# Which 128 keys make a chunk: every second token of 256, or every 26th token of all

## The chip, the cores and the metric

The kernel runs on one core of one Trainium2 chip. A core has a matrix engine (TensorE, PE in the profile), a vector engine (VectorE, DVE), an engine for activation functions (ScalarE, ACT), a general one (GpSimd, POOL), a queue that issues transfers (SyncE, SP), and 16 DMA engines that move data between the device memory and the on-chip memory SBUF. TensorE writes its results to PSUM. The metric is the device time of the launch in microseconds (us); the median of three runs of the kernel before is 10094.3 us (10090.54 to 10097.2).

## What is computed

Two graph layers on 3327 tokens of 128 features. Layer 0 is a graph attention layer over the 0/1 matrix `adj`. Layer 1 carries nearly all of the time:

```python
q = (x @ Wq.T).reshape(d, n, h)          # d = 128, n = 3327 tokens, h = 8
k = (x @ Wk.T).reshape(d, n, h)
v = (x @ Wv.T).reshape(d, n, h)
a = einsum('dnh,dmh->dnm', q, k) * scale + adj + adj
a = softmax(a, axis=2)                   # over the keys m
out = einsum('dnm,dmh->dnh', a, v)
x = layernorm(x + out.reshape(n, h * d) @ Wo.T)
```

So there are 128 independent attentions ("heads" in this text), each with 3327 queries, 3327 keys and only 8 numbers per query, key and value. For each one a table of 3327 x 3327 scores is made, `2 * adj` is added (or its exponential multiplied in), every element goes through an exponential, and the result is multiplied by the values. The sum over keys does not depend on the order in which the keys are taken.

## The kernel before, in words

**Tiling of layer 1.** The heads are taken four at a time (`HG = 4`), in 32 groups `g`. In a group the queries are cut into 7 blocks `b` of 476 (the last of 472). In a block the keys are cut into `NT = 26` chunks of up to 128 keys, one key to each of the 128 partitions; 25 chunks have 128 keys and the last has 127 (`kr`). Keys on partitions and queries along the row make a score tile of 128 x 476 for each of the four heads. That is 32 x 7 x 26 = 5,824 chunks of four heads.

**Which tokens a chunk holds.** Chunk `i` holds the tokens `i, i + 26, i + 52, ...`: partition `p` has token `26 p + i`. The keys `k4` of a group lie in SBUF as 32 rows (for each head: 8 features and their rounding errors, each twice) of 3327 tokens, and `scores` (lines 136 to 143) takes the slice `k4[..., i::NT]` of them as the stationary operand of a matmul, one element in every 26. The values `v4` lie with keys on partitions: partition `p` holds the 26 tokens from `26 p` on, 9 numbers each (8 values and a one for the sum), which is one run of 936 bytes of device memory per partition and head (`values`, lines 693 to 697). The adjacency tile `at` of a stretch of three chunks (`want_adj`, lines 722 to 743) takes two or three neighbouring rows of the transposed `adj` for each partition, 476 numbers of each row. [...]the transfers of the last chunk are cut by `_cut` into 112, 15 and 1 partitions.

**Rounds.** A stretch of three chunks `(i, i+1, i+2)` is worked on in three rounds (`rounds`, line 885 on). In each round TensorE makes four score tiles (four matmuls of 32 x 128 weights, one for each quarter of the rows of the array, L137), then up to eight matmuls of side work, and then the products with the values of a chunk of four rounds ago (`products`, L906: four matmuls, which the profile shows as eight). Two ways lead from scores to weights. For a chunk in `times` (the first of each stretch) ScalarE takes the exponential straight from PSUM (L1104, two heads, 952 columns) and GpSimd multiplies by a factor tile made of `adj` (L1105). For the other two VectorE adds `adj` (L1107, two heads) and ScalarE takes the exponential of four heads at a time in SBUF (L936, 1904 columns); for the last two chunks of the block it takes two heads at a time (`late`, lines 1110 to 1118). Per stretch ScalarE thus has two activations of 952 columns and two of 1904.

**Buffers and order.** The order of every engine is written out by hand (`tc.manual_schedule`); each engine runs its list in order and waits on semaphores. The score tiles of chunks in `times` have one PSUM buffer (`pe`), the others two (`pd`), the accumulated product one (`pv`), the weights `e4` seven. An adjacency tile is asked for three stretches before its use (`AHEAD = 3`) and there are five of them. In the first group (`RAW`, 63 stretches) all three chunks of a tile are loaded from `adj`, and GpSimd turns the first into a factor (`make_factor`, L750), which is stored (`ftd`); from then on the factor is loaded (L731) and only the other two chunks come from `adj` (L740). The loads all go through SP's queue. The keys and values of the next group are loaded in the last 18 rounds of a group (`OPEN`): the list `parts` has four transfers of keys and three of values, and its k-th is issued in round `18 k / len(parts)` of these. For the first group the values are loaded from ScalarE's queue. Layer 0, the projections and the final result are woven in as side work on TensorE, VectorE and GpSimd (`work_tensor`, `work`); they keep their own order of tokens (`p * NT + i`), as does the path `general`, which is not taken with this data.

Of the kernel before, what the change touches and what calls it, by code (L numbers as in the profile page):

```python
# [17 lines left out]
P = 128  # L18
# [16 lines left out]
def _ap(t, offset, dims):  # L35
    return bass.AP(tensor=t.tensor, offset=t.offset + offset, ap=[list(d) for d in dims])


def _cut(n):

    if n % 16 == 0:
        return [(0, n)]
    c = (n - 1) // 16 * 16
    return [(a, b) for a, b in ((0, c), (c, n)) if b > a]
# [3 lines left out]
def kernel(  # L48
# [27 lines left out]
    nc = tc.nc  # L76
    N, D = x.shape
    H = wqT.shape[1]
    assert D == P
    NT = -(-N // P)  # L80
    G = N * D
    H1 = H + 1
    H4 = 4 * H
# [4 lines left out]
    HG = 4  # L88
    NG = D // HG

    FP = N // NT
    kr = [FP + (i < N - FP * NT) for i in range(NT)]
    assert FP == P - 1
    REST = N - FP * NT
# [16 lines left out]
    vd = dram.tile([G + 1, H1], F32, name="vd")  # L111
# [12 lines left out]
    where = {i: (i % 3 if NT % 3 != 1 or i < NT - 1 else 1) for i in range(NT)}  # L124
# [6 lines left out]
    eps = const.tile([P, 1], F32, name="eps")  # L131
    nc.vector.memset(eps, EPS)
    flag = const.tile([1, 1], I32, name="flag")
    ALL = {ENG.PE, ENG.Activation, ENG.DVE, ENG.Pool, ENG.SP}

    def scores(dst, k4, q4, i, r, j, nb, stop=True):
        nc.tensor.matmul(  # L137
            dst,
            k4[32 * j : 32 * j + H4, i::NT],
            q4[32 * j : 32 * j + H4, :nb],  # L140
            start=True,
            stop=stop,
        )


    def special():
        with ExitStack() as sx, tc.manual_schedule(engines=ALL):
            keep = sx.enter_context(tc.tile_pool(name="sx_keep", bufs=1))
            bg2 = sx.enter_context(tc.tile_pool(name="sx_bg2", bufs=2))
# [95 lines left out]
            def tick(all_=False):  # L245
                for p in pend:
                    p[0] -= 1
                while pend and (all_ or pend[0][0] <= 0):
                    pend.pop(0)[1]()
# [431 lines left out]
            def open_group(g):  # L681

                k4 = kp.tile([P, N], F32R, name="k4b")
                v4 = kp.tile([P, HG, VW], F32, name="v4b")
                nc.gpsimd.memset(v4[:, :, REST * H1 :], 0.0)

                def keys(j, engine=nc.sync):
                    engine.dma_start(
                        k4[32 * j : 32 * j + H4, :].bitcast(F32),
                        _ap(kT, (g * HG + j) * N, [[G, 2 * H], [0, 2], [1, N]]),  # L690
                    )

                def values(p0, p1, k, engine=nc.sync):
                    engine.dma_start(
                        v4[p0:p1, :, : k * H1],
                        _ap(vd, (g * HG * N + p0 * NT) * H1, [[NT * H1, p1 - p0], [N * H1, HG], [1, k * H1]]),
                    )

                parts = [lambda j=j, **kw: keys(j, **kw) for j in range(HG)]
                for p0, p1, k in [c + (NT,) for c in _cut(FP)] + [(FP, P, REST)]:  # L700
                    parts.append(lambda c=(p0, p1, k), **kw: values(*c, **kw))
                return k4, v4, parts

            def open_queries(g, b):
# [17 lines left out]
            def want_adj(n):  # L722

                if n >= len(stretches):
                    return
                g, b, m = stretches[n]
                a = adjs[n] = ap_.tile([P, 3, WB], F32, name="at")
                n0, _, w = exact[b]
                cs = stretch[m]
                if n >= RAW and cs[0] in times:  # L730
                    nc.sync.dma_start(a[:, 0, :w], ftd[b][m][:, :w])  # L731
                    cs = cs[1:]
                z = where[cs[0]]
                there = sum(i < REST for i in cs)
                parts = [(0, P, there)]
                if there < len(cs):
                    parts = [c + (len(cs),) for c in _cut(FP)] + [(FP, P, there)]
                for p0, p1, k in parts:
                    if k:
                        nc.sync.dma_start(  # L740
                            a[p0:p1, z : z + k, :w],
                            _ap(adjT, (p0 * NT + cs[0]) * N + n0, [[NT * N, p1 - p0], [N, k], [1, w]]),
                        )

            def make_factor(n):
                if n < min(RAW, len(stretches)) and stretch[stretches[n][2]][0] in times:
# [10 lines left out]
            with ExitStack() as st:  # L757
# [40 lines left out]
                for m in range(AHEAD):  # L798
                    want_adj(m)
# [86 lines left out]
            for m, st_ in enumerate(stretch):  # L886
                starts[len(rounds)] = m
                if len(st_) > 1:
                    i = st_[0]
# [173 lines left out]
            for g in range(NG):  # L1063
                k4, v4, _ = group
                for b in range(NBLK):
                    s = Block()
                    s.g, s.b, s.q4, s.k4, s.v4, s.left, s.e, added = g, b, queries[0], k4, v4, NT, {}, {}
                    w = s.w = exact[b][2]
                    for n, rnd in enumerate(rounds):
                        at = b * NR + n  # L1070
                        if n in starts:
                            m = (g * NBLK + b) * NST + starts[n]
                            want_adj(m + AHEAD)
                            a = adjs[m]
                        tick()
                        if g + 1 < NG:
                            if at == total - OPEN:
                                finish_to(("rows", reads[g + 1]), None)
                                tick(True)
                                group = open_group(g + 1)  # L1080
                            for k, f in enumerate(group[2]):
                                if at >= total - OPEN and at == total - OPEN + OPEN * k // len(group[2]):
                                    f()
                        if n == NR // 2 and (b + 1 < NBLK or g + 1 < NG):
                            queries = open_queries(g, b + 1) if b + 1 < NBLK else open_queries(g + 1, 0)
                        for j in range(HG):
                            if n == NR // 2 + j * (NR > 12) and (b + 1 < NBLK or g + 1 < NG):
                                queries[1](j)
                        sc = []
                        for i, h in rnd:  # L1090
                            sc.append((pe if i in times else pd).tile([P, 2, 512], F32, name="scb"))
                            for t in range(2):
                                scores(sc[-1][: kr[i], t, :w], s.k4, s.q4, i, kr[i], 2 * h + t, w)
                        work_tensor(g * total + at, n)
                        for (i, h), z in zip(rnd, sc):
                            r = kr[i]
                            if i not in s.e:
                                s.e[i] = sp.tile([P, HG, WB], F32, name="e4")
                                added[i] = 0
                            eh = s.e[i][:r, 2 * h : 2 * h + 2, :w]  # L1100
                            added[i] += 1
                            ah = a[:r, where[i], :w].unsqueeze(1).to_broadcast([r, 2, w])
                            if i in times:
                                nc.scalar.activation(eh, z[:r, :, :w], AF.Exp, scale=2.0)  # L1104
                                nc.gpsimd.tensor_tensor(eh, eh, ah, op=ALU.mult)  # L1105
                            else:
                                nc.vector.tensor_tensor(eh, z[:r, :, :w], ah, op=ALU.add)  # L1107
                        now = g * total + at
                        exp_late(now)
                        for i, h in rnd:  # L1110
                            if i in times:
                                continue
                            if NT % 3 == 2 and i == NT - 1:
                                late.append((now + 2, s, i, 2 * h, 2 * h + 2))
                            elif NT % 3 == 2 and i == NT - 3:
                                late.append((now + 1 + h, s, i, 2 * h, 2 * h + 2))
                            elif added[i] == 2 and (now + 1, s, i, 0, HG) not in late:
                                late.append((now + 1, s, i, 0, HG))
                        if n + 1 in starts or n + 1 == NR:
                            del adjs[m]  # L1120
                            make_factor(m + 1)
                        waiting.append((s, order[n]))
                        while len(waiting) > LAG:
                            products(*waiting.pop(0))
                        work(g * total + at, n)
# [386 lines left out]
```

## Time and profile before

| | |
|---|---|
| median of three runs | 10094.3 us (10090.54 to 10097.2) |
| span of the profiled execution, first to last instruction | 10090.1 us |
| median less span (what lies around the span, and the spread of runs) | 4.2 us |
| busy: PE / DVE / ACT / POOL | 9904.1 / 9357.3 / 9969.7 / 9204.1 us (98 / 93 / 99 / 91%) |
| weight loads (PEld) | 3839.3 us, of them 2527.0 us for the scores (23,296 loads of 295 ns mean) |
| transfers | 1728.28 MB, mean 171 GB/s; 1,183,646 packets |
| granted TensorE clock, mean | 0.996 |

The profiled execution gives no time of its own besides its span. A busy time is the union of an engine's instructions. Matmuls are pipelined, and the ends that the profile gives them are modelled, so that a PE at 98% is not shown to be at its limit. A weight load (PEld) fills the stationary operand and may overlap with matmuls that are already running. ACT's instructions overlap by some 0.1 us where they follow one another at once, so that busy times of its groups sum to more than the engine's. All engines but the queue are over 90% busy, and the shares alone do not tell which of them sets the pace.

### The profile page before, as it was taken

How to read it: one execution, taken by the hardware profiler on the slowest of the kernel's cores; microseconds unless marked ns; L12 is line 12 of the kernel's file. 1: busy time of each engine (PE TensorE's matmuls, PEld its weight loads, DVE VectorE, ACT ScalarE, POOL GpSimd, SP SyncE). 2: the span in 40 equal slices, each digit the busy share in tenths (PEclk: the TensorE clock that was granted, in tenths of full speed). 3: DMA queues.
4: the chain of work that ended last, by engine and by line, in shares of the span. 5: the costliest groups of instructions: out<-in, count | busy, mean ns of one | idle time of the engine just before them, and what ended most of it. 6: DMA issues, size and time to landing. Idle time of an engine off the chain costs nothing.

```text
span 10090.1 us, 211982 instructions
## 1 busy us (share of the span) xinstructions
PE 9904.1 (98%) x81923; PEld 3839.3 (38%) x81923; DVE 9357.3 (93%) x11592; ACT 9969.7 (99%) x8352; POOL 9204.1 (91%) x4416
## 2 busy tenths in 40 slices
PE   8999999999999999999999999999999999999999
PEld 3333333333333333333333333333333333333333
DVE  7999999999999999989999999999999999998888
ACT  7999999999999999999999999999999999999998
POOL 7999999999999999989999999999999999998987
PEclk9999999999999999999999999999999999999999
DMA  7655555655655655655555665556555565555554
GB/s 202 199 170 173 171 171 173 179 171 167 176 162 176 180 157 176 176 166 175 166 170 173 181 177 163 162 175 176 175 174 165 162 177 175 174 159 169 165 166 123
DMA packets 1183646, 1728.28 MB, mean 171 GB/s; under 512 B 131527, under 2 KB 1171105, under 8 KB 1178527
## 3 DMA queue, kind: packets, MB, share of 16 engines
q1 hardware_dynamic: 1178484, 1712.02, 57.4%
q8 instruction: 644, 10.55, 0.4%
q14 instruction: 379, 3.10, 0.1%
q10 hardware_dynamic: 4139, 2.61, 0.1%
HBM read 1610.23 MB, written 103.93 MB: 170 GB/s over the span
## 4 chain that ended last, share of the span: by engine, by line
PE 79%; ACT 12%; DVE 4%; issue 2%; POOL 2%; DMA 1%; ACTq 0%; DVEq 0%; SPq 0%; POOLq 0%
PE av L906 40%; PE scb L137 33%; ACT e L936 6%; ACT e L1104 6%; PE bank L228 4%; DVE e L1107 2%; POOL e L1105 2%; DVE o L916 1%; PE bank L488 0%; DMA at<-ftd 0%; POOL at L750 0%; DVE ot L497 0%; DMA at<-in_adjT_dram 0%; DVE w L295 0%; DVE root L220 0%
## 5 line engine op out<-in xcount | busy, mean ns | idle before, releaser
L1105 POOL TENSOR_TENSOR e<-e,at 128x952 f32<-128x952 f32 (+1 forms) x4032 | 8958.8, 2235 | 803.1 <-ACT e L1104 729.1
L1107 DVE TENSOR_TENSOR e<-scb,at 128x952 f32<-128x952 f32 (+1 forms) x7616 | 8407.8, 1143 | 644.7 <-PE scb L137 333.6
L936 ACT ACTIVATE e<-e 128x1904 f32<-128x1904 f32 (+2 forms) x4256 | 6875.6, 1621 | 2.3 <-DVE e L1107 1.7
L906 PE MATMUL av<-e,v4b 128*32 128x476 f32 x46592 | 5870.3, 572 | 42.7 <-DVE o L916 27.2
L137 PE MATMUL scb<-q4b,k4b 32*128 32x476 f32 (+1 forms) x23296 | 4338.8, 592 | 105.7 <-ACT e L1104 35.4
L137 PEld LDWEIGHTS scb<-q4b,k4b 32*128 32x128 f32 (+1 forms) x23296 | 2527.0, 295 | 4770.4 <-issue 2638.3
L1104 ACT ACTIVATE e<-scb 128x952 f32<-128x952 f32 (+1 forms) x4032 | 3872.4, 960 | 66.4 <-PE scb L137 56.7
L906 PEld LDWEIGHTS av<-e,v4b 128*32 128x32 f32 x46592 | 1056.9, 108 | 1068.2 <-issue 611.0
L228 PE MATMUL bank<-hsb,w 128*32 128x129 f32 (+1 forms) x5200 | 278.0, 286 | 0.0
L313 DVE TENSOR_SCALAR_CACHE_REDUCE dump<-a 128x384 bf16<-128x384 f32 (+2 forms) x468 | 247.1, 528 | 0.6
L304 POOL TENSOR_TENSOR w<-w,a 128x384 f32<-128x384 f32 (+3 forms) x225 | 207.0, 920 | 0.1
L295 DVE TENSOR_SCALAR w<-trow,er 128x129 f32<-128x129 f32 x650 | 201.0, 338 | 0.0
L228 PEld LDWEIGHTS bank<-hsb,w 128*32 128x32 f32 (+1 forms) x5200 | 102.4, 108 | 148.3 <-issue 148.3
L916 DVE COPY o<-av 128x476 f32<-128x476 f32 (+1 forms) x224 | 145.8, 651 | 7.3 <-PE av L906 6.5
L393 DVE SCALAR_TENSOR_TENSOR lo<-bank,hi 128x128 fp32r<-128x128 f32 (+1 forms) x400 | 116.6, 292 | 13.8
L390 DVE TENSOR_SCALAR hi<-bank 128x128 fp32r<-128x128 f32 (+1 forms) x400 | 112.0, 280 | 0.0
L228 PE MATMUL bank<-wv,x1T 128*32 128x128 f32 x1600 | 85.2, 285 | 4.0 <-DVE vb L414 4.0
L228 PE MATMUL bank<-wk,x1T 128*32 128x128 f32 x1600 | 85.2, 285 | 0.0
L228 PE MATMUL bank<-wo,ot 128*32 128x128 f32 x1600 | 85.2, 285 | 0.0
L228 PE MATMUL bank<-wq,x1T 128*32 128x128 f32 x1600 | 85.2, 285 | 0.0
L414 DVE COPY vb<-bank 128x128 f32<-128x128 f32 (+1 forms) x200 | 56.2, 281 | 5.5 <-PE bank L228 5.5
L488 PE MATMUL bank<-ident,o 128*128 128x128 f32 x225 | 52.0, 304 | 0.0
(123 smaller groups left out, 659.9 us busy)
## 6 DMA issues: line engine op xcount, KB each, us to landing
at<-in_adjT_dram SPq DMA_DIRECT2D x1488, 476.0 KB
at<-ftd SPq DMA_DIRECT2D x1674, 238.0 KB
at<-in_adjT_dram SPq DMA_DIRECT2D x248, 472.0 KB
at<-ftd SPq DMA_DIRECT2D x279, 236.0 KB
k4b<-kT SPq DMA_DIRECT2D x128, 415.9 KB
q4b<-qT SPq DMA_DIRECT2D x1528, 29.8 KB
at<-in_adjT_dram SPq DMA_DIRECT2D x186, 208.2 KB
at<-in_adjT_dram SPq DMA_DIRECT2D x48, 714.0 KB
```

The costliest lines, as they stand in the source:

```text
L137: nc.tensor.matmul(dst, k4[32 * j : 32 * j + H4, i::NT], q4[32 * j : 32 * j + H4, :nb], start=True, stop=stop,)
L228: nc.tensor.matmul(dst[c0:c1], w[:, c0:c1], mov, **kw)
L295: nc.vector.tensor_scalar(w, s["t"][:, :, :T3], e, None, op0=ALU.max)
L304: nc.gpsimd.tensor_tensor(w, w, s["a"][n][:, c0 - i0 : c1 - i0, :r], op=ALU.mult)
L313: nc.vector.tensor_scalar(z, a, float(k), None, op0=ALU.is_equal, op1=ALU.add, accum_out=even[:, t, at : at + 1])
L393: nc.vector.scalar_tensor_tensor(lo[:r, o : o + QW], s["b"][:r, :QW], scale, hi[:r, o : o + QW].bitcast(F32), op0=ALU.mult, op1=ALU.subtract,)
L906: nc.tensor.matmul(s.av[32 * j : 32 * j + 32, : s.w], s.v4[:r, j, i * H1 : i * H1 + 32], e[:r, j, : s.w], start=(s.left == NT - 1), stop=( ...
L916: nc.vector.tensor_copy(o4[:, :w], s.av[:, :w])
L936: nc.scalar.activation(e, e, AF.Exp, scale=2.0)
L1104: nc.scalar.activation(eh, z[:r, :, :w], AF.Exp, scale=2.0)
L1105: nc.gpsimd.tensor_tensor(eh, eh, ah, op=ALU.mult)
L1107: nc.vector.tensor_tensor(eh, z[:r, :, :w], ah, op=ALU.add)
```

## The change

A chunk of the path `special` now holds every second token of a window of 256. Chunks `2 j` and `2 j + 1` share the tokens from `256 j` on: the even ones go to chunk `2 j`, the odd ones to `2 j + 1`; `first_key(i)` is the chunk's first token. Sizes are as before: 25 chunks of 128 keys and one of 127. `pair_scores` slices the keys in steps of 2 in place of steps of 26. The values of chunks 0 to 23 are loaded by four transfers, one per head, in which a partition collects 12 runs of 18 numbers (72 bytes); those of chunks 24 and 25 by three more (`last_values`: 112, 15 and 1 partitions, 72 bytes per partition and head, 36 in the last). The list of parts of a group thus grows from 7 to 11. The adjacency tile takes its rows to match; where three chunks are loaded (in the first group), it is one transfer for the first and one for the other two, in place of one for the three. The instructions of TensorE, VectorE and GpSimd, and the activations, are the same in number, size and order as before.

```diff
@@ -131,6 +131,12 @@
     eps = const.tile([P, 1], F32, name="eps")
     nc.vector.memset(eps, EPS)
     flag = const.tile([1, 1], I32, name="flag")
+    assert NT % 2 == 0 and N == NT * P - 1
+
+    def first_key(i):
+
+        return i // 2 * 2 * P + i % 2
+
     ALL = {ENG.PE, ENG.Activation, ENG.DVE, ENG.Pool, ENG.SP}
 
     def scores(dst, k4, q4, i, r, j, nb, stop=True):
@@ -144,6 +150,15 @@
 
 
     def special():
+        def pair_scores(dst, k4, q4, i, r, j, nb):
+            nc.tensor.matmul(
+                dst,
+                k4[32 * j : 32 * j + H4, first_key(i) : first_key(i) + 2 * r - 1 : 2],
+                q4[32 * j : 32 * j + H4, :nb],
+                start=True,
+                stop=True,
+            )
+
         with ExitStack() as sx, tc.manual_schedule(engines=ALL):
             keep = sx.enter_context(tc.tile_pool(name="sx_keep", bufs=1))
             bg2 = sx.enter_context(tc.tile_pool(name="sx_bg2", bufs=2))
@@ -682,7 +697,7 @@
 
                 k4 = kp.tile([P, N], F32R, name="k4b")
                 v4 = kp.tile([P, HG, VW], F32, name="v4b")
-                nc.gpsimd.memset(v4[:, :, REST * H1 :], 0.0)
+                nc.gpsimd.memset(v4[:, :, (NT - 1) * H1 :], 0.0)
 
                 def keys(j, engine=nc.sync):
                     engine.dma_start(
@@ -690,15 +705,24 @@
                         _ap(kT, (g * HG + j) * N, [[G, 2 * H], [0, 2], [1, N]]),
                     )
 
-                def values(p0, p1, k, engine=nc.sync):
+                def values(j, engine=nc.sync):
+                    k = NT // 2 - 1
                     engine.dma_start(
-                        v4[p0:p1, :, : k * H1],
-                        _ap(vd, (g * HG * N + p0 * NT) * H1, [[NT * H1, p1 - p0], [N * H1, HG], [1, k * H1]]),
+                        v4[:, j, : k * 2 * H1].rearrange("p (a e) -> p a e", e=2 * H1),
+                        _ap(vd, (g * HG + j) * N * H1, [[2 * H1, P], [2 * P * H1, k], [1, 2 * H1]]),
+                    )
+
+                def last_values(p0, p1, k, engine=nc.sync):
+                    i = NT - 2
+                    engine.dma_start(
+                        v4[p0:p1, :, i * H1 : (i + k) * H1],
+                        _ap(vd, (g * HG * N + i * P + 2 * p0) * H1, [[2 * H1, p1 - p0], [N * H1, HG], [1, k * H1]]),
                     )
 
                 parts = [lambda j=j, **kw: keys(j, **kw) for j in range(HG)]
-                for p0, p1, k in [c + (NT,) for c in _cut(FP)] + [(FP, P, REST)]:
-                    parts.append(lambda c=(p0, p1, k), **kw: values(*c, **kw))
+                parts += [lambda j=j, **kw: values(j, **kw) for j in range(HG)]
+                for c in [c + (2,) for c in _cut(FP)] + [(FP, P, 1)]:
+                    parts.append(lambda c=c, **kw: last_values(*c, **kw))
                 return k4, v4, parts
 
             def open_queries(g, b):
@@ -730,17 +754,25 @@
                 if n >= RAW and cs[0] in times:
                     nc.sync.dma_start(a[:, 0, :w], ftd[b][m][:, :w])
                     cs = cs[1:]
-                z = where[cs[0]]
-                there = sum(i < REST for i in cs)
-                parts = [(0, P, there)]
-                if there < len(cs):
-                    parts = [c + (len(cs),) for c in _cut(FP)] + [(FP, P, there)]
-                for p0, p1, k in parts:
-                    if k:
-                        nc.sync.dma_start(
-                            a[p0:p1, z : z + k, :w],
-                            _ap(adjT, (p0 * NT + cs[0]) * N + n0, [[NT * N, p1 - p0], [N, k], [1, w]]),
-                        )
+                for of in [cs[:-2], cs[-2:]] if len(cs) > 2 else [cs]:
+                    if not of:
+                        continue
+                    z = where[of[0]]
+                    step = first_key(of[-1]) - first_key(of[0])
+                    full = sum(kr[i] == P for i in of)
+                    parts = [(0, P, full)]
+                    if full < len(of):
+                        parts = [c + (len(of),) for c in _cut(FP)] + [(FP, P, full)]
+                    for p0, p1, k in parts:
+                        if k:
+                            nc.sync.dma_start(
+                                a[p0:p1, z : z + k, :w],
+                                _ap(
+                                    adjT,
+                                    (first_key(of[0]) + 2 * p0) * N + n0,
+                                    [[2 * N, p1 - p0], [(step or 1) * N, k], [1, w]],
+                                ),
+                            )
 
             def make_factor(n):
                 if n < min(RAW, len(stretches)) and stretch[stretches[n][2]][0] in times:
@@ -1090,7 +1122,7 @@
                         for i, h in rnd:
                             sc.append((pe if i in times else pd).tile([P, 2, 512], F32, name="scb"))
                             for t in range(2):
-                                scores(sc[-1][: kr[i], t, :w], s.k4, s.q4, i, kr[i], 2 * h + t, w)
+                                pair_scores(sc[-1][: kr[i], t, :w], s.k4, s.q4, i, kr[i], 2 * h + t, w)
                         work_tensor(g * total + at, n)
                         for (i, h), z in zip(rnd, sc):
                             r = kr[i]
```

## The prediction

> **What bounds the kernel now.** I read the page first: busy times, then the chain that ended last.
>
> ```profile
> PE 9904.1 (98%) x81923; PEld 3839.3 (38%) x81923; DVE 9357.3 (93%) x11592; ACT 9969.7 (99%) x8352; POOL 9204.1 (91%) x4416
> ...
> PE 79%; ACT 12%; DVE 4%; issue 2%; POOL 2%; DMA 1%; ACTq 0%; DVEq 0%; SPq 0%; POOLq 0%
> ```
>
> Two engines look full, and the chain names PE. But the chain follows an engine's own instructions back as long as nothing shows a release, and PE's ends are modelled. So next the timeline of ScalarE, to see whether it ever pauses (start, duration, instruction):
>
> ```profile
> 4535.78 1.79 ACT L936 ACTIVATE e<-e 128x1904 f32<-128x1904 f32 x1
> 4537.46 0.96 ACT L1104 ACTIVATE e<-scb 128x952 f32<-128x952 f32 x1
> 4538.32 0.99 ACT L936 ACTIVATE e<-e 128x952 f32<-128x952 f32 x1
> 4539.34 0.96 ACT L1104 ACTIVATE e<-scb 128x952 f32<-128x952 f32 x1
> ...
> 4541.98 0.99 ACT L936 ACTIVATE e<-e 127x952 f32<-127x952 f32 x1
> 4542.87 0.95 ACT L1104 ACTIVATE e<-scb 128x952 f32<-128x952 f32 x1
> ```
>
> Each activation starts before the one ahead has ended. A start that nothing delays comes 1.68 us after a 1904-column one, 0.84 to 0.86 us after L1104, 0.89 us after a 952-column L936 (the last pair). The one at 4539.34 comes after 1.02 us: 0.13 us late without any idle time in the record. I took all start-to-start distances of the two activation lines from the trace and their lower quartile per kind (1681, 843, 844, 888, 886 ns). These floors sum to 9,843 us of the 10,001 us from the first exponential to the end of the last. **ScalarE is at 98.4% of its floor**, which the change leaves alone. Late starts for which PE's scores are the releaser sum to 94.4 us: 25.0 before 420 us, and 69.4 us over 713 starts after.
>
> Then how PE and ACT wait for each other, and what a group of scores is made of (waits; timeline of PE; weight loads by shape, with busy us and mean ns):
>
> ```profile
> PEld scb L137 <- ACT e L1104: 1881.9, 2245, 1.5
> ...
> ACT e L1104 <- PE scb L137: 56.7, 39, 20.4
> ```
>
> ```profile
> 5002.49 0.60 PE L137 MATMUL scb<-q4b,k4b 32*128 32x476 f32 x4
> 5003.02 0.42 PE L228 MATMUL bank<-wq,x1T 128*32 128x128 f32 x8
> ```
>
> ```profile
> L137 PEld LDWEIGHTS scb<-q4b,k4b 32*128 32x128 f32 x22400 | 2477.6, 295 | 4769.8 <-issue 2638.3 <-ACT e L1104 1881.9 <-DVE dump L313 63.7
> L906 PEld LDWEIGHTS av<-e,v4b 128*32 128x32 f32 x44800 | 995.4, 108 | 1002.7 <-issue 565.2 <-POOL e L1105 347.9 <-DVE o L916 68.9
> ...
> L488 PEld LDWEIGHTS bank<-ident,o 128*128 128x128 f32 x225 | 23.5, 140 | 28.4 <-issue 28.2 <-DMA q4b<-qT 0.2
> ```
>
> In 2,245 of its score groups PE stood before the load until ACT had emptied the one buffer `pe`; ACT had idle time for PE only 39 times, 20.4 us of it at the start. An undelayed group takes 0.53 us (5002.49 to 5003.02), of which the four parallel loads, issued together, are 0.295 us: exposed, not hidden. A load of 128 neighbouring columns takes 140 ns (L488). Last, engines by stretch (busy PE, PEld, DVE, ACT, POOL; clock; DMA share; GB/s):
>
> ```profile
> 64.00:420.00 356.00, 332.37 (x2725) 121.53 (x2725) 314.82 (x400) 331.58 (x274) 341.45 (x211) 0.97 0.72 208
> 420.00:9960.00 9540.00, 9434.42 (x78317) 3655.71 (x78316) 8917.07 (x10965) 9522.22 (x7933) 8768.40 (x4152) 1.00 0.58 171
> ```
>
> In the first group GpSimd, which also makes factors, is fullest (341 of 356 us): lateness there isn't PE's to give back. After it ACT has 9,522 of 9,540.
>
> [...]
>
> **The change part by part.**
>
> 1. Weight loads of the scores, 295 ns [...]. I take 140 ns, the row for neighbouring columns[...]. Saving 155 ns per score group; 5,824 groups make 903 us of PE time. Nearly all of it becomes longer waiting for ACT's release. What counts are the late starts of ACT: capping each of the 713 at 155 ns leaves 56.3 of 69.4 us. Another 27.5 us of late starts after 1904-column activations carry no releaser or ACT's own; half may be the same cause: 14 us. In the first group, 3 of 25 us. Gain 73 us (ends: 0 at 295 ns; 27.7 us if only 50 ns are saved; some 92 us if every block came to the quickest seen, 44.02 us against the median's 44.45, over 214 blocks).
> 2. Values of a group: 6,652 packets of 72 bytes and 4 of 36, for 508 of 936 bytes and 4 of 900: 416 per DMA engine for 32. The trace has no 72-byte packet; its means are 12.9 ns for 104 bytes, 18.6 for 172, 30.6 for 512, 57.8 for 936. I take 18.6[...]: 7.7 for 1.8 us, +5.9 us per engine and group (ends: +3.5 at 12.9, +10.9 at 30.6). It falls into the only stretch where DMA is already full:
>
> ```profile
> 9709.00:9740.00 31.00, 30.59 (x228) 11.02 (x220) 28.50 (x33) 31.00 (x25) 27.52 (x14) 1.00 0.95 237
> ```
>
> What hides it is the lead of the adjacency loads queued behind. From the semaphores of the trace, a factor load issued in a group's last 35 us lands in 3 to 6 us (at most 9.1), and its first use comes 8.8 us or more after landing, in nine of ten 11 us. The values are issued in ten rounds, and in the last 20 us of a group DMA is 80% busy (mean over 25 changes of groups, from the packets), so some 4 us fit in anyway. +5.9 and +10.9 both stay under 8.8 + 4. Cost 0, 1 us allowed. If the cover were gone, `at` would be late for GpSimd and VectorE, then ScalarE.
> 3. Keys are issued in rounds 0 to 4 of the window for 0 to 7 (11 parts for 7): same bytes, earlier, behind the same slack. Four parts more on SP at 0.6 us, SP being idle between waits for VectorE: 0.
> 4. First group: 56 stretches have one more `at` issue at 0.43 us, 24 us of SP over 356; GpSimd's first chunk lands no later. Same rows, bytes and 1904-byte packets; the rows lie nearer together. 0, allow 1 us (end: 6 us at the change of groups near 370 us, where SP is crowded).
> 5. Start: four more issues on ScalarE's queue, 0.6 us each, 2.4 us; the last is now issued near 58 us, the first exponential is at 63.7. Allow 2 us.
>
> Sum: -73 + 4 = -69 us against the span, 10,021; the 4.2 us around it stay: **10,025 us**.
>
> **Rivals.** (a) PE is the bound, as the chain says: -903 us, 9,190. Against it: ACT's floor of 9,843 cannot be undercut. 2%. (b) All lateness goes: -92 + 4, 10,006. For it: blocks of 44.02 us exist; against: VectorE's side work also delays releases. 18%. (c) Step 2 isn't read faster, or hardly: 10,066 at 50 ns saved (6%), and 10,094 to 10,098 at none (9%). Nothing in the trace excludes it. (d) Slower: the 72-byte packets. One mechanism: from about 35 ns per packet ((8.8 + 4 + 1.8) us / 416) the backlog eats the lead; at 41 ns, 2.4 us of stall in each of 31 groups cancel the gain. At 60 ns: 25.0 - 14.6 = 10.4 us x 31 = 320 us, 10,345. Against it: even 512-byte packets take 30.6 ns; for it: the window is at 0.95. 9%.
>
> **How the numbers follow.** Likeliest case 56%, with its own range 9,998 to 10,060. Differences under 0.2% (20 us) can't be told from none. Faster: 56 + 18 + 2 + 5 of the 6 of the half effect = 0.81; same 0.10; slower 0.09. The range 9,995 to 10,090 takes in the likeliest case, most of (b) and (c); (a), (d) and the rest of no change stay out.
>
> **What would show it.** [...]the undelayed group at 0.35 to 0.4 us; ACT's wait rows for PE nearly gone, the stretch from 420 us on shorter by 60 to 90 us with ACT as full as before; PE's busy time down by hundreds of us, its wait for L1104 up. Packets of 72 bytes under 25 ns. Wrong would be: loads near 295; `at` transfers as releasers of POOL or DVE at each change of groups; a first group longer by over 6 us.

## The result, and the profile after

The changed kernel takes 10004.8 us (median, 10003.6 to 10009.4) against 10095.2 us of the kernel before, run beside it: a ratio of 0.9911 with a 95% interval of 0.9897 to 0.9926, or 90 us less. The forecast was 10,025 us, 69 us less.

The page of the kernel after, engines and chain, as shown for the kernel before:

```profile
PE 9461.4 (95%) x81923; PEld 3078.5 (31%) x81923; DVE 9334.1 (93%) x11592; ACT 9892.4 (99%) x8352; POOL 9201.7 (92%) x4416
...
ACT 40%; PE 24%; POOL 16%; issue 11%; DVE 6%; DMA 2%; SPq 1%; POOLq 0%; ACTq 0%; DVEq 0%
```

PE's busy time is down by 443 us, the span by only 87. The chain, which went through PE for 79% of its length, is now a mixture led by ScalarE. The scores' weight loads by line, and the waits between PE and ACT (us in total, times, longest us; L154 is the new slice, L1136 the exponential from PSUM that was L1104):

```profile
L154 PEld LDWEIGHTS scb<-q4b,k4b 32*128 32x128 f32 (+1 forms) x23296 | 1764.2, 189 | 5371.8 <-ACT e L1136 3489.9
```

```profile
PEld scb L154 <- ACT e L1136: 3489.9, 3768, 2.4
...
PE scb L154 <- ACT e L1136: 370.8, 1428, 2.0
...
ACT e L1136 <- PE scb L154: 33.8, 19, 5.2
```

A load takes 189 ns where it took 295. What PE saved it now spends standing before ScalarE: the wait in front of the load grew from 1881.9 to 3489.9 us, and matmuls too wait now, 370.8 us for 35.4 us before. ScalarE's row for PE, which was forecast to be nearly gone, hardly moved: of the 56.7 us before, 20.4 were the start, which now stands in another row (22.8 us for the values' transfers), and the 33.8 us left compare with 36.3. The timeline of PE (start, duration, instruction, idle time before it):

```profile
4962.51 0.50 PE L154 MATMUL scb<-q4b,k4b 32*128 32x476 f32 x4 [0.27 <-ACT e L1136]
4962.94 0.42 PE L243 MATMUL bank<-wq,x1T 128*32 128x128 f32 x8
```

A group of scores that nothing delays takes 0.43 us in place of 0.53, as much less as the load's 106 ns, and PE visibly idles before it. The timeline of ScalarE at the end of a block, where the start shown in the prediction had been 0.13 us late:

```profile
4502.67 1.10 ACT L968 ACTIVATE e<-e 128x952 f32<-128x952 f32 x1
4503.56 1.07 ACT L1136 ACTIVATE e<-scb 128x952 f32<-128x952 f32 x1
```

0.89 us from start to start, the floor of this kind. Records of ACT are some 50 ns longer than before while the floors of the distances between starts are the same within 1 ns, so it is the distances that count. Last, the window of the groups after the first (columns as before: length; busy PE, PEld, DVE, ACT, POOL; clock; DMA share; GB/s):

```profile
420.00:9870.00 9450.00, 9007.25 (x78297) 2924.21 (x78293) 8892.57 (x10964) 9445.31 (x7931) 8763.77 (x4149) 1.00 0.61 172
```

ScalarE is busy for 9,445 of 9,450 us, PE for 9,007. Cut at the first exponentials of blocks, the 87 us of the span lie here: start to the first exponential 63.7 to 65.9 us, the first eight blocks 381.0 to 380.4, the next 213 blocks 9477.9 to 9391.0, the end 167.4 to 165.8. The median block fell from 44.45 to 44.11 us. The summed lateness of ScalarE's starts over their floors fell from 156.0 to 74.3 us.

### The profile page after: what moved, and what is told of

Same layout as the page of the kernel before. It is cut to its first block, busy times and chain, and to the rows that moved or that the text cites. A ratio compares the mean times of both kernels' runs of the same rounds, so it can differ in the third digit from the quotient of the medians.

```text
span 10003.1 us, 212173 instructions
## 1 busy us (share of the span) xinstructions
PE 9461.4 (95%) x81923; PEld 3078.5 (31%) x81923; DVE 9334.1 (93%) x11592; ACT 9892.4 (99%) x8352; POOL 9201.7 (92%) x4416
## 2 busy tenths in 40 slices
DMA packets 1383200, 1728.31 MB, mean 173 GB/s; under 512 B 347463, under 2 KB 1370657, under 8 KB 1378079
## 4 chain that ended last, share of the span: by engine, by line
ACT 40%; PE 24%; POOL 16%; issue 11%; DVE 6%; DMA 2%; SPq 1%; POOLq 0%; ACTq 0%; DVEq 0%
ACT e L968 25%; POOL e L1137 16%; ACT e L1136 15%; PE scb L154 12%; PE av L938 11%; DVE e L1139 4%; PE bank L243 1%; DVE o L948 1%; DVE lo L408 0%; DMA q4b<-qT 0%; POOL w L319 0%; DMA at<-ftd 0%; DVE hi L405 0%; DMA k4b<-kT 0%; DVE w L310 0%
## 5 line engine op out<-in xcount | busy, mean ns | idle before, releaser
L968 ACT ACTIVATE e<-e 128x1904 f32<-128x1904 f32 (+2 forms) x4256 | 7104.0, 1678 | 2.0 <-DVE e L1139 1.6
L154 PE MATMUL scb<-q4b,k4b 32*128 32x476 f32 (+1 forms) x23296 | 3749.2, 486 | 442.8 <-ACT e L1136 370.8
L1136 ACT ACTIVATE e<-scb 128x952 f32<-128x952 f32 (+1 forms) x4032 | 4078.6, 1012 | 57.5 <-PE scb L154 33.8
L154 PEld LDWEIGHTS scb<-q4b,k4b 32*128 32x128 f32 (+1 forms) x23296 | 1764.2, 189 | 5371.8 <-ACT e L1136 3489.9
```

What stands on the lines that cost most here:

```text
L154: nc.tensor.matmul(dst, k4[32 * j : 32 * j + H4, first_key(i) : first_key(i) + 2 * r - 1 : 2], q4[32 * j : 32 * j + H4, :nb], start=True, ...
L968: nc.scalar.activation(e, e, AF.Exp, scale=2.0)
```

## The experiments

Times are medians; the kernel before, beside them, took 10,094 to 10,096 us.

**The slice alone: steps of 2, 1 and 4.** Values, adj and all else as in the kernel before.

```diff
-                k4[32 * j : 32 * j + H4, i::NT],
+                k4[32 * j : 32 * j + H4, k0 : k0 + STEP * (r - 1) + 1 : STEP],
# STEP 2: k0 = i // 2 * 2 * P + i % 2
# STEP 1: k0 = i * P
# STEP 4: k0 = min(i // 4 * 4 * P + i % 4, N - 1 - 4 * (r - 1))
```

> The kernel before with the key slice of the scores alone changed to every second token of 256; values and adj still belong to every 26th token, so the weights are applied to the wrong keys. If the weight load is the whole cause of the gain, a load takes 189 ns and the time is that of the changed kernel or up to 5 us less (9,998 to 10,006). If the new loads of values and adj helped too (rows nearer together), this run stays 10 us or more above it.

> The kernel before with the key slice alone changed to 128 neighbouring tokens (wrong keys for the values and adj, as above). [...]this load takes the same 189 ns as step 2 and the time is equal. If it goes by the bytes that are spanned, [...]the time falls by at most 25 us more, since only about 31 us of late starts of ScalarE were left after 420 us: 9,980 to 10,000.

> The kernel before with the key slice alone changed to every fourth token of 512 (16 bytes apart; wrong keys for the values and adj, as above). [...]this load takes the 295 ns of step 26 and the time is that of the kernel before, 10,090 to 10,100. If the load's time grows with the step, it lies between 189 and 295 ns, say 220, and the time between 10,005 and 10,060.

Measured: step 2 10003.6 us (ratio 0.991, 0.9894 to 0.9927), step 1 10000.9 (0.9907, 0.989 to 0.9923), step 4 10131.2 (1.0037, 1.0023 to 1.0051). The weight loads by shape, of step 1 and of step 4 (there L151 is the changed slice, L1116 the exponential from PSUM):

```profile
L151 PEld LDWEIGHTS scb<-q4b,k4b 32*128 32x128 f32 x22400 | 1656.9, 182 | 5412.0 <-ACT e L1116 3522.2 <-issue 1412.1 <-DVE e L1119 242.8
```

```profile
L151 PEld LDWEIGHTS scb<-q4b,k4b 32*128 32x128 f32 x22400 | 2530.3, 303 | 4759.2 <-issue 2636.3 <-ACT e L1116 1881.3 <-DVE dump L325 63.7
```

Step 2 alone gives the whole gain: the new way of loading values and adj has no part in it. Step 1 is hardly better than step 2 (182 ns for 189), and step 4 is as bad as step 26 (303 for 295). Both loads came out within 8 ns of the first case expected for them. The times did not all follow: step 4 was expected at the time of the kernel before, and its 8 ns more cost 36 us, while the 3 us between steps 2 and 1 lie within the spread of their runs. The clock tells the two kinds of load apart as well: where the trace shows a granted clock of 0.5, loads of step 1 and 2 take 283 ns (median of 64 in each run), those of step 26 and 4 take 295 and 303 (48 each), as at the full clock. So at steps 26 and 4 the load takes as long at a clock of 0.5 as at 1, while at steps 1 and 2 it takes about half as much again (283 ns for 182 and 189).

**The loads alone.** The changed kernel with the old slice.

```diff
-                                pair_scores(sc[-1][: kr[i], t, :w], s.k4, s.q4, i, kr[i], 2 * h + t, w)
+                                scores(sc[-1][: kr[i], t, :w], s.k4, s.q4, i, kr[i], 2 * h + t, w)
```

> The changed kernel with the old key slice (every 26th token), values and adj loaded in the new way, so that again weights and keys do not belong together. If the new transfers cost nothing, this equals the kernel before within 5 us, 10,090 to 10,100, with loads of 295 ns. If the 72-byte packets cost something that the faster load hid, it is slower than before by that: 10,105 or more.

10097.4 us, ratio 1.0003 (0.9995 to 1.0012): no difference that can be measured. The 199,554 packets more (1,383,200 for 1,183,646) cost no time that shows.

**Two more doses.** Step 3 in every chunk; step 2 in one chunk of three, the other two with step 26.

```diff
+            if i % 3 != 2:
+                scores(dst, k4, q4, i, r, j, nb)
+                return
```

> The kernel before with every third token of 384 as the key slice (wrong keys for values and adj). [...]from 189 ns[...] and 303[...] I estimate 246 ns. Mean pace with a floor: all of the gain, 10,000 to 10,010. Late starts capped at what one load saves, 49 ns (the way the prediction counted): 10,055 to 10,070.

> The kernel before with every second token of 256 as the key slice in one chunk of three alone (the third of each stretch), the other two still every 26th token; weights and keys do not belong together. Loads are 189 ns in a third of the rounds, so TensorE saves 35 ns a round on the average. If TensorE's mean pace was the bound and ScalarE's floor comes some 13 ns a round below it (0.34 us per block of 26 rounds), a third of the loads gives all or nearly all of the gain: 10,003 to 10,025. If each late start of ScalarE has to be mended in its own round, it gives about a third of it: 10,055 to 10,075.

Step 3 took 10022.0 us (0.9926, 0.991 to 0.9943), the third 10045.1 us (0.9951, 0.9934 to 0.9967). The load of step 3:

```profile
L151 PEld LDWEIGHTS scb<-q4b,k4b 32*128 32x128 f32 x22400 | 2150.9, 246 | 4992.1 <-ACT e L1116 3207.9 <-issue 1430.3 <-DVE e L1119 193.7
```

246 ns is what was expected, midway between the loads of step 2 (189) and step 4 (303). The load does not go on growing with the step: at step 26 it takes 295 ns, less than at step 4. Both times lie between the two expectations. Mean load against time:

| mean load, ns | 303 | 295 | 262 (8 chunks of 26) | 246 | 189 | 181 |
|---|---|---|---|---|---|---|
| time, us | 10131 | 10095 | 10045 | 10022 | 10004 | 10001 |
| us per ns to the next | 4.5 | 1.5 | 1.4 | 0.3 | 0.4 | |

Were PE alone the bound, a nanosecond in each of the 5,824 groups would be worth 5.8 us. It is over three quarters of that above 295 ns (one run), a quarter of it down to 246, and a fifteenth or so below that; the last step, from 189 to 181, can't be told from nothing. In the column for 262 ns the fast loads stand only in rounds in which no score goes to the single buffer `pe`, so its mean isn't the same dose as an even 262. By these points the kernel before stood on the knee.

**Which engine was the bound.** 40 of 476 queries are left out of the exponential in SBUF, in the kernel before and in the changed one; these keep their raw scores.

```diff
-                    e = s.e[i][: kr[i], h0:h1, : s.w]
+                    e = s.e[i][: kr[i], h0:h1, : s.w - 40]
```

> The kernel before with ScalarE's load lightened: the exponential in SBUF (L936) leaves out the last 40 of 476 queries of every head, which keep their raw scores. That takes 160 of 1904 columns, by the floors of the trace 0.88 ns each or 141 ns, from 3,360 activations and 70 ns from 896: some 537 us of ScalarE's time. If ScalarE's floor alone sets the pace before, the time falls by 200 us or more, to 9,890 or less, until VectorE is full. If TensorE with its slow loads is as tight as ScalarE, which the run with 303 ns loads speaks for, the time falls by less than 80 us: 10,015 or more.

> The changed kernel with the same 40 of 476 queries left out of the exponential in SBUF. With loads of 189 ns TensorE has some 617 us more room than before, so ScalarE sets the pace alone and the time falls by 200 us or more, to 9,800 or less, until VectorE is full. If something else is as tight as ScalarE (the single buffer of scores, GpSimd), it falls by less than 100 us: 9,905 or more.

Before: 10084.6 us, ratio 0.9989 (0.9982 to 0.9996), 11 us less. After: 9606.3 us, 0.9515 (0.9499 to 0.9531) of the kernel before, that is 398 us less than the changed kernel. Windows of the lightened kernel before and of the lightened changed one:

```profile
420.00:9900.00 9480.00, 9366.24 (x77909) 3622.75 (x77913) 8865.71 (x10911) 9142.57 (x7890) 8714.43 (x4130) 1.00 0.57 171
```

```profile
420.00:9450.00 9030.00, 8892.31 (x78117) 2910.64 (x78113) 8730.51 (x10929) 9005.62 (x7912) 8717.59 (x4140) 1.00 0.63 180
```

In the first, ScalarE has 337 us of idle time, PE as little as ever. The waits of the lightened kernel before show for whom ScalarE waits (56.7 us in this row before):

```profile
ACT e L1104 <- PE scb L137: 316.3, 1277, 19.9
```

The floors of ScalarE's starts sum to 9,337 us there in place of 9,843, so 506 us of work were taken out (537 were forecast), and the lateness grew from 156 to 658 us, 611 of it behind PE's scores. **With loads of 295 ns the ring through TensorE (the load, the scores, the engine that empties their buffer, the next load) set the pace, and ScalarE, with its floor only a little lower, was kept just busy.** With loads of 189 ns it is ScalarE: lightened by about as much, it pulls the time down by 398 us.

**How far the transfers are from hurting.** Three kernels put more packets in front of the adjacency loads. `contiguous` is the whole kernel with 128 neighbouring tokens per chunk; `thrice` fetches the values three times into the same tile; `spare` fetches them three times, the copies into tiles of their own.

The main added lines of each:

```diff
# contiguous
+        return i * P
+                        _ap(vd, (g * HG + j) * N * H1, [[H1, P], [P * H1, k], [1, H1]]),
+                            _ap(adjT, (first_key(cs[c0]) + p0) * N + n0, [[N, p1 - p0], [P * N, k], [1, w]]),
# thrice
+                    for _ in range(1 if g == 0 else 3):
+                        values(j, **kw)
# spare
+                    for v, c in [(v4, j)] + [(spare[0], j), (spare[1], j % 2)] * (g > 0):
```

> The whole kernel with chunks of 128 neighbouring tokens, adj to match, and values in runs of 36 bytes: 13,308 packets a group in place of 6,656. The load takes 181 ns as in the run with the slice alone, worth nothing beyond 189. If transfers stay hidden, 10,000 to 10,008, as the changed kernel. If the doubled number of packets (832 per engine at 11 ns, 9.2 us in place of 5.2) breaks through the lead of the adjacency loads, 10,030 or more.

> The changed kernel, in which each transfer of values of chunks 0 to 23 is issued three times over from the second group on (the same data): 12,288 packets of 72 bytes more a group, or some 9.7 us of every engine at 12.6 ns. The least time from the landing of a factor tile to its use is 6.0 us in the changed kernel, and nine of ten have 7.5 us. If this lead is what hides the values, most of it is used up: up to 2 us of stall a group, 10,005 to 10,070, with DMA as the releaser of GpSimd or VectorE. If nothing queues behind the values, 10,000 to 10,008.

> The changed kernel with the values of chunks 0 to 23 fetched three times from the second group on, the copies into spare tiles of their own, so that no issue has to wait for an earlier one to land (the third copies of heads 2 and 3 go over those of heads 0 and 1, several rounds later). 1,184 packets of 72 bytes per engine and group in place of 416, 14.9 us in place of 5.2. If the stall of 18 us a group with three copies in one tile came from SP waiting for landings, it is gone or small here: 10,000 to 10,060. If it came from the packets, it stays: 10,400 or more.

Measured: `contiguous` 10010.1 us (0.9918, 0.9901 to 0.9934); its 213 blocks take 9388.2 us against 9391.0 of the changed kernel, while its first exponential starts at 72.9 us for 65.9. Twice the packets of values (13,308 for 6,656 a group) cost no time that shows in these blocks. At the start, where the values come over ScalarE's own queue and four of their issues take 10.7 us in place of 3.8, 7 us are lost, which puts the run 2 us above what was expected. `thrice`: 10581.2 us (1.0478, 1.0461 to 1.0496). The waits of SP's queue in `thrice` (L710 loads values), and those of the engines (L1144 is VectorE's addition of `adj`, L1142 GpSimd's product):

```profile
SPq L710 <- DMA v4b<-vd: 795.4, 248, 8.5
```

```profile
DVE e L1144 <- DMA at<-in_adjT_dram: 552.7, 64, 15.7
...
POOL e L1142 <- DMA at<-ftd: 425.2, 68, 11.2
```

Each copy into the same tile waits on the queue until the one before has landed, 248 times, and with it waits every adjacency load behind. So this run tells nothing about packets, and the expectation had overlooked those waits. `spare` takes them away: 10128.1 us (1.0036, 1.0022 to 1.005), 123 us over the changed kernel, 4.0 us in each of 31 groups. Its SP queue has no such row, and VectorE still waits (L1142 is its addition here):

```profile
DVE e L1142 <- DMA at<-in_adjT_dram: 115.9, 46, 6.7
```

That is more than the 60 us at most that was expected, and far from the 400 of a stall by packets alone: some 450 of the 576 us of `thrice` go away with the waiting on the queue, and the rest comes after the lead has been used up. The limit lies between 9.2 us of values per engine and group (`contiguous`, no stall) and 14.9 (`spare`); the changed kernel has 5.2. These are packets per engine times what one takes in the changed kernel, so the first two are estimates: 832 of 36 bytes at 11 ns, 1,184 of 72 bytes at 12.6, and 416 of 72 bytes. By the semaphores, the least time from the landing of a factor tile to its use, near a change of groups, is 6.0 us in the changed kernel, 2.2 in `contiguous` and 0.1 in `spare`.

Not all of the 123 us is waiting for transfers. Two windows of `spare` at a change of groups (columns as before; the DMA share adds up the packets' times and can pass 1), the wait for `at` and what follows it:

```profile
1036.00:1041.70 5.70, 2.78 (x22) 0.57 (x17) 2.10 (x4) 3.41 (x4) 5.70 (x4) 1.00 1.17 196
1041.70:1048.50 6.80, 6.17 (x38) 1.85 (x42) 4.52 (x6) 4.51 (x4) 2.81 (x2) 0.50 1.03 306
```

In the first window PE is busy for 2.78 of 5.70 us at a granted clock of 1.00; in the second, of 6.8 us, the clock is 0.50. Over the whole run ScalarE's exponential from PSUM waits 73.2 us for PE's scores, 33.8 us in the changed kernel. Between 390 us and some 250 us before the end, `spare` has 150 us at a clock of 0.5, in 23 stretches near changes of groups, and `thrice` 672 us; the changed kernel has 3.4. What share of the 123 us this is was not separated; if all work went at half speed in those 150 us, they would cost 75 us, which is an estimate of the most it can be.

## Why the prediction was right, and where it was not

**What bounds the kernel now: wrong in its first half.** The step "ScalarE is at 98.4% of its floor", read as what sets the pace, failed. The lightened kernel before refutes it: 506 us of ScalarE's work taken out gave 11 us, where the faster loads gave 90. The chain of the page, which the prediction set aside because PE's ends are modelled, named the right engine. ScalarE's floor rightly excluded the 9,190 us of rival (a), but it tells how much can be gained, not who leads. An engine at 98.4% may be the second one. Right was that the floor ends the gain after 1%: PE saved 106 ns in each of 5,824 groups, 617 us, of which 90 came out.

Which part of the ring is tightest was not separated. In the timeline from 5000.77 us, a stretch of 5.07 us holds two score groups of 0.78 and 0.73 us where an undelayed one takes 0.53, since the second pair of loads waits for VectorE's release; so PE was not full in the sense of never waiting, and handing over to VectorE belongs to the ring. So does ScalarE's exponential from PSUM, which the lightened kernel left as it was.

**Part 1, weight loads: the size was off twice, in opposite ways.** The load takes 189 ns, not 140: the row for 128 columns side by side (L488) is of full-height tiles, and 32-row tiles take 181 ns even with neighbouring tokens. That step 2 would load as fast as neighbouring columns was the author's estimate; the trace of the kernel before has no load of step 2. The saving was 106 ns, not 155. The gain in lateness was 81.7 us, not 73, and the floors themselves came out 7 us lower in sum (1 ns or so per start). By kind, late starts behind PE's scores fell by 36.9 us (94.4 to 57.5), those after 1904-column activations with no releaser or ACT's own by 27 us (27.5 to under 1), of which the prediction allowed half, and those of L936 after L1104 with no releaser by 20.6 us (30.0 to 9.4), which it had left out. Capping each late start by what one load saves was the wrong account: step 3 with 49 ns saved gave 72 us of the 90, not 28. That delays pass on from round to round would explain it, which no run shows by itself. The result landed at rival (b)'s 10,006, where every block comes to the quickest seen, 44.02 us: the median block came to 44.11. Not all lateness went; 74.3 us are left. That the forecast lies only 21 us off is in part luck: it took too much off a load and let too little of that reach ScalarE.

**Parts 2 to 4, transfers: right.** Packets of 72 bytes took 12.6 ns on the average (forecast 18.6), so 5.2 us per engine and group. The least time from landing to use of a factor tile issued in a group's last 35 us fell from 8.8 to 6.0 us; nothing stalled, and the loads alone cost nothing measurable. The point from which rival (d) decides was put at 14.6 us of values per engine and group; with 14.9 the loss is already 4 us a group, an unseparated part of it at a clock of 0.5, so the cover ends earlier, near 11 as an estimate (the 5.2 of the changed kernel and the 6.0 left over; `contiguous`, with 9.2 and 2.2, gives the same). Part 3 and part 4 show in no row; the first eight blocks are 0.6 us shorter.

**Part 5, the start: right.** 2.2 us later, 2 were allowed.

## What to carry to other kernels

Take the floor of a busy engine as a limit on the gain, but find the leader by lightening one engine at a time: two engines within 1% of each other both look full, and only one of them pays for work taken out. Choose which rows or tokens make a tile so that the stationary operand is read at a small step: here loads of step 1 and 2 took 181 and 189 ns, step 3 246, steps 4 and 26 303 and 295. Let the transfers gather the rest, as long as the lead of the loads queued behind covers them (no stall at 9.2 us of values per engine and group, 4 us a group lost at 14.9). The same nanosecond was worth most of its full price on one side of the knee (4.5 of 5.8 us) and next to nothing on the other (0.3), so measure more than one size.

## What the runs showed that was not expected

The load at step 26 is 8 ns shorter than at step 4 (295 and 303), at step 1 it is 8 ns shorter than at step 2 (181 and 189), and 114 ns lie between steps 2 and 4; why is open. In `thrice` a transfer that overwrites what an unfinished one writes held the whole issuing queue: 795 us of queue waits in a kernel that took 576 us more. The weight load for a quarter of the array's rows, four of them issued together, takes 181 ns for 128 columns at best, where the full-height load took 140. At a granted clock of 0.5 the fast loads take 283 ns and the slow ones their 295 or 303. And `spare` has 23 stretches of 3 to 10 us at a clock of 0.5 near changes of groups; the one shown follows 5.70 us in which PE was busy for 2.78.
